# A graph layer on one core: open segments in two parts, half of the first gate moved up, six PSUM banks and the gate ahead of the numerators in the last pass

## The chip, the core and the metric

The kernel runs on one core of one Trainium2 chip. Its engines are TensorE (matrix products into PSUM, eight banks of 128 x 512 f32), VectorE, ScalarE, GpSimd and SyncE (SP), which here only issues transfers; GpSimd issues the indirect transfers and some plain ones, ScalarE some plain ones. 16 DMA engines move the data. The metric is the device time of one execution in microseconds (us). The kernel's time before is 2014.91 us, the median of three runs (2013.11 to 2015.74).

## What is computed

A graph layer over 1250 nodes of 1024 features and 20000 edges of 8 types, then a feed-forward part; all in f32.

```python
xn = _layernorm(x)
# graph part: per relation a mean over a node's edges, then a matrix
out = xn @ root + bias
for r in range(8):
    mask = (edge_type == r)
    sums = segment_sum(xn[src] * mask[:, None], dst, N)
    cnt = segment_sum(mask, dst, N)
    out = out + (sums / maximum(cnt, 1.0)[:, None]) @ weight[r]
u = out
z = concatenate([u, xn], axis=1) @ w_gate + b_gate
gnn = tanh(u) * z + xn * (1.0 - z)
# mixing part: linear attention, 8 heads of 16, features 1, q, q (x) q
normed = rms_norm(xn, gamma); q, k, v = normed @ w_q, normed @ w_kv
mix = ((phi(q) @ (phi(k).T @ v)) / maximum(phi(q) @ sum(phi(k)), 1e-5)) @ w_out
x = x + gnn + mix
# feed-forward part with FP4 quantized operands (blocks of 16)
xq = quant(_layernorm(x))
h = silu(xq @ quant(f_gate).T) * (xq @ quant(f_up).T)
x = x + quant(h) @ quant(f_down).T
```

## The kernel before

The nodes are worked in ten blocks (`NB`) of 128 rows (`BR`), the last of 98. The features are worked in two halves of 512 columns (`HD`). All of it is unrolled; each engine takes its instructions in a fixed order that a scheduler made of the program.

1. Up to about 1483 us: layer norm, sorting of the edges by node (L224 to L391), and the products of all nodes with all relation matrices, `y_d` in DRAM, then `root_d`, `gx_d` (the second half of the gate's product, with `xn`) and `qkv_d`. Beside the products run the messages.
2. A message tile (`message`, L604; `gather`, L459; `segments`, L466) is 128 sorted edges: GpSimd gathers 128 rows of `y_d` (four `msg` buffers), ScalarE and VectorE weight them and split them into two parts (`hi`, `lo`), TensorE sums equal nodes with two products (L477, L478), ScalarE copies the sum (L479) and writes it to `seg_d` (L480). There are 157 tiles (`ST`) for each half. The second half has 23 gathers left when the products end.
3. The end of the messages (the loop at L835): beside the last ones stand the sums of the mixing part (`mix_sums`, `mix_pairs`, ending in `bd`, L743), `open_rows` (which tile's last row belongs to a node that goes on in the next tile), and `open_segments` (L805), which adds these last rows to the row of the tile in which the node ends: row 127 of each tile is loaded (`last_rows`, L797; 128 rows in `s1`, 29 in `s2`), multiplied by a selection (`osel`), evacuated (`osum`) and added in DRAM by an indirect transfer (L813), in two pieces of 128 and 29 rows. For half 0 that is done among the messages, for half 1 after them (L859). `behind` (L827) is a list of loads on GpSimd's queue: `x`, `root`, `gx` of block 0, the 4 MB of `wg`, the same three of block 1; one is taken after each step from the fourth on. `FW` = 6 quantized weight tiles are loaded meanwhile, on ScalarE's queue.
4. The numerators (`mix_num`, L663): for a block, `q` transposed, four products with `bd` (L673) into four PSUM tiles, each multiplied and reduced on VectorE (L676, L678), a fifth product (L680, L681), and the division (L690); `mix_transposed` (L693) turns the result. `FIRST` = 4 of them are made before block 0, among the transposes of the weights (`ffn_weight`, L817).
5. `block(b)` (L869): the node rows `u` are gathered from both halves of `seg_d` (`nodes`, L658), `root_d` is added (L887, L896), `u` is transposed (L160, copies L90), the gate is 16 products (L893, L904), the mixing part's output two (L907); then the sum, layer norm and quantizing (`x1`, `x2`). Block 0 takes the halves apart. `hidden` (L921) and `finish` (L938) are the feed-forward part. The last pass (L950) runs, for each i, a numerator ahead, `block(i)`, `hidden(i-1)`, `finish(i-2)`.

PSUM: `sg`, two banks, for messages (`sm_tile`); `mm`, four banks (`mm_tile`) for all products; `tr`, two banks for transposes. `tc.issue_after(ins)` keeps what follows behind `ins` on its engine. `loaded[b]` has two buffers for each of `xt`, `rt`, `gx` and `u`.

Of the kernel before, what the change touches and what calls it, by code (L numbers as in the profile page):

```python
# [8 lines left out]
F32 = mybir.dt.float32  # L9
# [18 lines left out]
FIRST = 4  # L28
LAG = 2
EARLY = 140  # L30
FW = 6
SUMS = 7
# [17 lines left out]
def gps_layer(ctx: ExitStack, tc: tile.TileContext, x, src, dst, et, w_rel, w_root, bias,  # L50
# [9 lines left out]
    def psum_pools(stack, **bufs):  # L60
        for name, n in bufs.items():
            psum[name] = stack.enter_context(tc.tile_pool(name=f"ps_{name}", bufs=n, space=PSUM))
# [12 lines left out]

    def mm_tile():
        return psum["mm"].tile([128, 512], F32, name="mm")
# [388 lines left out]
    def segments(nh, t, msg):  # L466
# [13 lines left out]
        S.dma_start(seg_d[nh][t * 128:(t + 1) * 128, :], seg)  # L480
# [29 lines left out]
    psum_pools(ctx, sg=2)  # L510
# [123 lines left out]
    qn = mx.tile([BR, NB, 128], F32, name="qn")  # L634
# [64 lines left out]

    with ExitStack() as late:  # L700
        op = late.enter_context(tc.tile_pool(name="op", bufs=1))
        pb = late.enter_context(tc.tile_pool(name="pb", bufs=4))
        fw = late.enter_context(tc.tile_pool(name="fw", bufs=6))
        kv = op.tile([BR, NB, 257], F32, name="kv")
# [3 lines left out]
        for o, c0, c in ((kv, 128, 384), (qn, 0, 128)):  # L708
            nc.sync.dma_start(o[:, :NB - 1, :c - c0], qkv_d[:full, c0:c].rearrange("(b p) c -> p b c", p=BR))
            nc.sync.dma_start(o[:rest_n, NB - 1, :c - c0], qkv_d[full:, c0:c])  # L710
# [86 lines left out]
        def last_rows(nh):  # L797
            s1 = op.tile([128, HD], F32, name="s1")
            s2 = op.tile([128, HD], F32, name="s2")
            rows127 = seg_d[nh][:ZERO, :].rearrange("(t p) c -> t p c", p=128)[:, 127, :]  # L800
            G.dma_start(s1, rows127[:128])
            G.dma_start(s2[:B2], rows127[128:])
            return s1, s2

        def open_segments(nh, s1, s2):  # L805
            for i, n in enumerate((128, B2)):
                ps = mm_tile()
                T.matmul(ps[:n], osel[:, 0, i * 128:i * 128 + n], s1, start=True, stop=(i == 0))
                if i == 1:
                    T.matmul(ps[:n], osel[:B2, 1, 128:], s2[:B2], start=False, stop=True)  # L810
                osum = op.tile([128, HD], F32, name="osum", bufs=2)
                evac(osum[:n], ps[:n])
                G.indirect_dma_start(  # L813
                    out=seg_d[nh][:, :], out_offset=bass.IndirectOffsetOnAxis(ap=orow[:n, i:i + 1], axis=0),
                    in_=osum[:n, :], in_offset=None, compute_op=ALU.add)
# [16 lines left out]
        rest = [mix_sums, open_rows, lambda: open_segments(0, *last_rows(0))]  # L832
        rest += [lambda b=b: mix_pairs(b) for b in range(NB)]
        done = EARLY
        for i, p in enumerate(rest):  # L835
# [4 lines left out]
            if i >= 3:  # L840
                behind.pop(0)()
                if len(there) < FW:
                    there.append(ffn_weight(S, *weights[len(there)]))
# [9 lines left out]
        with tc.issue_after(gathered_last[0]):  # L853
            for b in range(2):
                nodes(b, 0)
            rows = last_rows(1)
        for p in steps[:SUMS]:
            p()
        open_segments(1, *rows)  # L859
# [9 lines left out]
    def block(b):  # L869
# [13 lines left out]
        if b == 0:  # L883

            for nh, cs in halves:
                with tc.issue_after(first_nums if nh else gathered_last[0]):
                    V.tensor_tensor(u[:, cs], rt[:, cs], u[:, cs], ALU.add)  # L887
                transpose_cols(uT[:, nh * 4:nh * 4 + 4, :], u[:, cs], n, D_CHUNKS[:4], 0)
                for mh, ms in halves:
                    if nh == 0:  # L890
                        gates.append(mm_tile())
                    for k in range(4 * nh, 4 * nh + 4):
                        T.matmul(gates[mh][:n], uT[:, k, :n], wg[:, k, ms], start=(k == 0), stop=(k == KC - 1))  # L893
# [97 lines left out]
```

## Time and profile before

| | |
|---|---|
| runs, median of three | 2014.91 us |
| profiled execution, whole / span | 2007.39 / 2005.6 us |
| mean granted TensorE clock | 0.968 |
| busy, share of the span | TensorE 95%, VectorE 65%, ScalarE 37%, GpSimd 30% |
| last gather of a message issued | 1561.92 us |
| last write of `seg_d` by ScalarE | 1574.13 us |
| `bd` made (L743) | 1572.16 + 0.69 us |
| block 0: last gate product ends | about 1626.2 us |
| `hidden` of block 0 / 1 / 2 / 3 begins (transposes of `x2`) | 1664.17 / 1699.06 / 1740.15 / 1781.05 us |
| span after the last gate of block 9 | 50.5 us |

A row of the timeline is start, length, engine, line, operation, tiles out and in, shapes, count; in brackets how long the engine stood idle before it and what ended that. An f32 product of 128x512 shows as two rows (x16 are eight products). A wait for several things is put down to the one that came last by the profile, which can be the wrong one where a transfer is among them. TensorE rows are modelled, so busy shares of TensorE say less than its gaps.

### The profile page before, as it was taken

What the parts mean: (1) busy time and instruction counts of PE and PEld (TensorE: products, weight loads), DVE (VectorE), ACT (ScalarE), POOL (GpSimd) and SP (SyncE); (2) the same over time, 40 slices, a digit from 0 to 9 for tenths busy, and PEclk for the clock granted to TensorE, in tenths of its full rate; (3) what the DMA queues carried; (4) which work ended last, traced back from release to release, by engine and by line L of the source; (5) the groups of instructions that cost most, each with busy time, mean ns of one, the idle gap of its engine ahead of it and who ended that gap; (6) DMA issues with size and microseconds to landing.
All of it is one profiled execution on the core that took longest, in us unless ns stands there. A gap on an engine that the chain in (4) does not pass through costs nothing. (4 is left out here: it accounts for less than half of the span.)

```text
span 2005.6 us, 24060 instructions
## 1 busy us (share of the span) xinstructions
PE 1900.6 (95%) x7828; PEld 1283.0 (64%) x7828; DVE 1310.8 (65%) x2931; ACT 751.3 (37%) x1302; POOL 611.6 (30%) x590
## 2 busy tenths in 40 slices
PE   8999999999999999999999989989988889989998
PEld 5465447787777777777777866767653334444544
DVE  8988946767646455645554675675656776676665
ACT  5111421112234545555554555555543332222311
POOL 1022588884012322332323334233344201000100
PEclk9999999999999999999999989999887879999999
DMA  6265334444346767677767677778688521211100
GB/s 215 79 160 150 77 89 125 115 117 124 120 155 212 229 220 232 215 236 226 227 212 221 222 252 254 235 235 263 227 302 305 146 80 55 76 63 61 56 21 29
DMA packets 159256, 332.76 MB, mean 166 GB/s; under 512 B 27006, under 2 KB 35876, under 8 KB 159130
## 3 DMA queue, kind: packets, MB, share of 16 engines
q0 software_dynamic: 39616, 112.32, 21.4%
q10 hardware_dynamic: 77370, 142.68, 19.2%
q1 hardware_dynamic: 42144, 76.22, 12.0%
q8 instruction: 62, 1.02, 0.2%
q14 instruction: 64, 0.52, 0.1%
HBM read 184.42 MB, written 146.53 MB: 165 GB/s over the span
## 5 line engine op out<-in xcount | busy, mean ns | idle before, releaser
L546 PE MATMUL ab<-wH,xH 128*128 128x512 f32 (+2 forms) x1440 | 568.0, 395 | 2.0 <-ACT wH L505 2.0
L547 PE MATMUL ab<-wL,xL 128*128 128x512 f32 (+2 forms) x1440 | 564.6, 393 | 0.0
L548 PE MATMUL ab<-wD,xD 128*128 128x512 f32 (+2 forms) x1440 | 561.2, 394 | 2.6 <-DVE wD L507 1.9
L461 POOL DMA_INDIRECT msg<-y_d,key x314 | 318.6, 1014 | 675.0 <-PE sm L478 337.5
L474 DVE SCALAR_TENSOR_TENSOR msg<-msg,weight,hi 128x512 fp32r<-128x512 f32 x314 | 234.4, 750 | 135.9 <-ACT hi L472 77.6
L548 PEld LDWEIGHTS ab<-wD,xD 128*128 128x128 f32 (+1 forms) x1440 | 268.2, 187 | 74.6 <-DVE wD L507 10.2
L546 PEld LDWEIGHTS ab<-wH,xH 128*128 128x128 f32 (+1 forms) x1440 | 269.5, 187 | 64.7 <-ACT wH L505 3.5
L547 PEld LDWEIGHTS ab<-wL,xL 128*128 128x128 f32 (+1 forms) x1440 | 269.3, 187 | 63.8 <-DVE wL L506 0.4
L479 ACT COPY seg<-sm 128x512 f32<-128x512 f32 x314 | 182.1, 584 | 204.3 <-PE sm L478 159.5
L472 ACT ACTIVATE hi<-msg,weight 128x512 fp32r<-128x512 f32 x314 | 222.1, 721 | 72.4 <-DMA msg<-y_d,key 30.0
L387 POOL DMA_INDIRECT sort_d<-pay,row x160 | 211.0, 1319 | 60.8 <-issue 48.4
L554 ACT ACTIVATE yt<-ab 128x512 f32<-128x512 f32 (+2 forms) x180 | 106.0, 592 | 320.9 <-PE ab L547 275.7
L555 DVE SCALAR_TENSOR_TENSOR yt<-ab,yt 128x512 f32<-128x512 f32 (+2 forms) x180 | 121.8, 681 | 155.7 <-ACT yt L554 148.2
L405 PE MATMUL mm<-wt,xnT 128*128 128x512 f32 (+1 forms) x480 | 221.3, 603 | 0.0
L478 PE MATMUL sm<-msg,sel 128*128 128x512 f32 x314 | 137.4, 438 | 24.2 <-DVE msg L474 24.0
L477 PE MATMUL sm<-hi,sel 128*128 128x512 f32 x314 | 133.2, 428 | 26.2 <-ACT hi L472 20.3
L470 DVE TENSOR_SCALAR sel<-iota_n,last_row 128x128 fp32r<-128x128 f32 x314 | 89.4, 287 | 103.8 <-PE sm L478 98.8
L405 PEld LDWEIGHTS mm<-wt,xnT 128*128 128x128 f32 (+1 forms) x480 | 85.5, 188 | 86.6 <-issue 86.3
L505 ACT CAST wH<-h 128x512 fp32r<-128x512 f32 x144 | 88.5, 621 | 123.5 <-DVE h L504 112.3
L904 PE MATMUL mm<-wg,uT 128*128 128x512 f32 (+1 forms) x288 | 131.6, 611 | 0.2 <-ACT uT L90 0.2
L506 DVE TENSOR_TENSOR wL<-raw,h 128x512 fp32r<-128x512 f32 x144 | 98.3, 683 | 27.2 <-PE mm L405 27.2
L659 POOL DMA_INDIRECT u<-seg_d,node_at x20 | 25.6, 1281 | 276.3 <-issue 244.8
(276 smaller groups left out, 2100.3 us busy)
## 6 DMA issues: line engine op xcount, KB each, us to landing
seg_d<-seg ACTq DMA_DIRECT2D x314, 256.0 KB
y_d<-yt ACTq DMA_DIRECT2D x144, 256.0 KB
raw<-in_L_gnn_weight_dram SPq DMA_DIRECT2D x104, 256.0 KB
db<-in_dst_dram POOLq DMA_DIRECT2D x32, 305.2 KB
xt<-in_x_dram SPq DMA_DIRECT2D x16, 512.0 KB
wt<-in_L_gnn_weight_dram SPq DMA_DIRECT2D x24, 256.0 KB
msg<-y_d,key POOLq DMA_INDIRECT x314
lb<-lo_d POOLq DMA_DIRECT2D x32, 156.2 KB
```

What stands on the lines that cost most here:

```text
L387: st = G.indirect_dma_start(out=sort_d[:, :], out_offset=bass.IndirectOffsetOnAxis(ap=row[:, t:t + 1], axis=0), in_=pay[:, t, :], in_offse ...
L405: T.matmul(ps[:n], xnT[:, k, block_rows(b)], held[k], start=(k == 0), stop=(k == KC - 1))
L461: gathered_last[0] = G.indirect_dma_start(out=msg[:, :], out_offset=None, in_=y_d[nh][:, :], in_offset=bass.IndirectOffsetOnAxis(ap=key[:, ...
L472: S.mul(hi, msg, weight[:, t:t + 1])
L474: V.scalar_tensor_tensor(lo, msg, weight[:, t:t + 1], hi.bitcast(F32), op0=ALU.mult, op1=ALU.subtract)
L477: T.matmul(ps, sel, hi, start=True, stop=False)
L478: T.matmul(ps, sel, lo, start=False, stop=True)
L479: S.copy(seg, ps)
L546: T.matmul(pa[:p, :n], xH[:, k, ns], Wh[:, :n], start=(k == 0), stop=False)
L547: T.matmul(pa[:p, :n], xL[:, k, ns], Wl[:, :n], start=False, stop=(k == KC - 1))
L548: T.matmul(pb[:p, :n], xD[:, k, ns], Wd[:, :n], start=(k == 0), stop=(k == KC - 1))
L904: T.matmul(gates[nh][:n], uT[:, k, :n], wg[:, k, cs], start=(k == 0), stop=(k == KC - 1))
```

## The change

- PSUM: the pool of the messages (`sg`) stands on the other side; after block 0 it is closed and its two banks become a pool `more`; from then on every third `mm_tile` comes from it.
- `qn` and `kv` become one tile `qkv`, loaded by two transfers instead of four; it stays to the end. `FW` 6 to 5, `FIRST` 4 to 3, `SUMS` 7 to 5.
- The open segments: `open_first` adds the piece of 128 rows for both halves among the messages; the adds to half 1 and the writes of tiles beyond 128 are declared independent. `open_rest` adds the piece of 29 rows (its last row is zero, 28 are loaded); for half 1 that is all that is left after the messages.
- `gate_first`: after `open_rest(1)`, the first half of block 0's `u` is added, transposed and multiplied with its half of `wg`, into the two `sg` banks; `block(0)` adds the second half.
- The loads in `behind` stay behind the message gathered last.
- Last pass: `block(i)` stands ahead of the numerator; the numerators are 3 to 9, one behind each of blocks 1 to 7.

```diff
-FIRST = 4
+FIRST = 3
-FW = 6
-SUMS = 7
+FW = 5
+SUMS = 5
...
+    banks = [0]
+
     def mm_tile():
-        return psum["mm"].tile([128, 512], F32, name="mm")
+        banks[0] += 1
+        return psum["more" if "more" in psum and banks[0] % 3 == 0 else "mm"].tile([128, 512], F32, name="mm")
...
-        S.dma_start(seg_d[nh][t * 128:(t + 1) * 128, :], seg)
+        wrote = S.dma_start(seg_d[nh][t * 128:(t + 1) * 128, :], seg)
+        if nh == 1 and t > 128:
+            tc.declare_no_dep(wrote.ins, group="open", reason="these are added to rows of tiles up to 128, and of waste")
...
-    psum_pools(ctx, sg=2)
+    sums = ctx.enter_context(ExitStack())
+    psum_pools(sums, "right", sg=2)
...
-    qn = mx.tile([BR, NB, 128], F32, name="qn")
+    qkv = mx.tile([BR, NB, 385], F32, name="qkv")
+    qn, kv = qkv[:, :, :128], qkv[:, :, 128:]
...
+    first_gates = []
+
+    def gate_half(nh, u, uT):
+
+        n, cs = BR, halves[nh][1]
+        transpose_cols(uT, u[:, cs], n, D_CHUNKS[:4], 0)
+        for ps, (_, ms) in zip(first_gates, halves):
+            for k in range(4):
+                T.matmul(ps[:n], uT[:, k, :n], wg[:, 4 * nh + k, ms], start=(nh + k == 0), stop=(nh + k == 4))
+
+    def gate_first():
+
+        first_gates.extend(sm_tile() for _ in range(2))
+        _, rt, _, u = loaded[0]
+        with tc.issue_after(gathered_last[0]):
+            V.tensor_tensor(u[:, :HD], rt[:, :HD], u[:, :HD], ALU.add)
+        gate_half(0, u, mx.tile([128, 4, BR], F32, name="uT0"))
...
-        for o, c0, c in ((kv, 128, 384), (qn, 0, 128)):
-            nc.sync.dma_start(o[:, :NB - 1, :c - c0], qkv_d[:full, c0:c].rearrange("(b p) c -> p b c", p=BR))
-            nc.sync.dma_start(o[:rest_n, NB - 1, :c - c0], qkv_d[full:, c0:c])
+        nc.sync.dma_start(qkv[:, :NB - 1, :384], qkv_d[:full, :].rearrange("(b p) c -> p b c", p=BR))
+        nc.sync.dma_start(qkv[:rest_n, NB - 1, :384], qkv_d[full:, :])
...
-        def last_rows(nh):
-            s1 = op.tile([128, HD], F32, name="s1")
-            s2 = op.tile([128, HD], F32, name="s2")
-            rows127 = seg_d[nh][:ZERO, :].rearrange("(t p) c -> t p c", p=128)[:, 127, :]
-            G.dma_start(s1, rows127[:128])
-            G.dma_start(s2[:B2], rows127[128:])
-            return s1, s2
-
-        def open_segments(nh, s1, s2):
...
+        s1, s2 = {}, [op.tile([128, HD], F32, name=f"s2{nh}") for nh in range(2)]
+        for nh in range(2):
+            V.memset(s2[nh][:B2], 0.0)
+
+        def open_add(nh, i, n, ps):
+            osum = op.tile([128, HD], F32, name="osum", bufs=2)
+            evac(osum[:n], ps[:n])
+            return G.indirect_dma_start(
+                out=seg_d[nh][:, :], out_offset=bass.IndirectOffsetOnAxis(ap=orow[:n, i:i + 1], axis=0),
+                in_=osum[:n, :], in_offset=None, compute_op=ALU.add).ins
+
+        def open_first(nh):
+            s1[nh] = op.tile([128, HD], F32, name="s1")
+            G.dma_start(s1[nh], rows127(nh)[:128])
+            ps = mm_tile()
+            T.matmul(ps, osel[:, 0, :128], s1[nh], start=True, stop=True)
+            added = open_add(nh, 0, 128, ps)
+            if nh == 1:
+                tc.add_to_no_dep_group("open", added)
+
+        def open_rest_rows(nh):
+
+            G.dma_start(s2[nh][:B2 - 1], rows127(nh)[128:ST - 1])
+
+        def open_rest(nh):
+            ps = mm_tile()
+            T.matmul(ps[:B2], osel[:, 0, 128:], s1[nh], start=True, stop=False)
+            T.matmul(ps[:B2], osel[:B2, 1, 128:], s2[nh][:B2], start=False, stop=True)
+            open_add(nh, 1, B2, ps)
...
-        rest = [mix_sums, open_rows, lambda: open_segments(0, *last_rows(0))]
+        rest = [mix_sums, open_rows, lambda: (open_first(0), open_rest_rows(0), open_rest(0), open_first(1))]
...
-                behind.pop(0)()
+                with tc.issue_after(gathered_last[0]):
+                    behind.pop(0)()
...
-            rows = last_rows(1)
+            open_rest_rows(1)
         for p in steps[:SUMS]:
             p()
-        open_segments(1, *rows)
+        open_rest(1)
+        gate_first()
...
         if b == 0:
-
-            for nh, cs in halves:
...
+            gates = first_gates
+            with tc.issue_after(first_nums):
+                V.tensor_tensor(u[:, HD:], rt[:, HD:], u[:, HD:], ALU.add)
+            gate_half(1, u, uT)
...
     for i in range(NB + 2):
-        if 0 < i and i + FIRST <= NB:
-            if i + FIRST < NB:
-                mix_num(i + FIRST)
-            mix_transposed(i + FIRST - 1)
         if i < NB:
             ahead[i] = block(i)
         if i == 0:
-            mix_num(FIRST)
-            mix_transposed(FIRST - 1)
+            sums.close()
+            psum_pools(ctx, "right", more=2)
+        if i and i + FIRST - 1 < NB:
+            mix_num(i + FIRST - 1)
+        if i and i + FIRST - 2 < NB:
+            mix_transposed(i + FIRST - 2)
```

More of the change, by code (lines that the diff above doesn't have):

```diff
@@ L58, in gps_layer, with psum_pools @@
     psum = {}
-    def psum_pools(stack, **bufs):
+    def psum_pools(stack, side="left", **bufs):
         for name, n in bufs.items():
-            psum[name] = stack.enter_context(tc.tile_pool(name=f"ps_{name}", bufs=n, space=PSUM))
+            psum[name] = stack.enter_context(tc.tile_pool(name=f"ps_{name}", bufs=n, space=PSUM, side=side))
     HD = D // 2
@@ L702, in gps_layer @@
         pb = late.enter_context(tc.tile_pool(name="pb", bufs=4))
-        fw = late.enter_context(tc.tile_pool(name="fw", bufs=6))
-        kv = op.tile([BR, NB, 257], F32, name="kv")
+        fw = late.enter_context(tc.tile_pool(name="fw", bufs=FW))
         V.memset(kv[:, :, 256:257], 1.0)
         full, rest_n = (NB - 1) * BR, N - (NB - 1) * BR
-        for o, c0, c in ((kv, 128, 384), (qn, 0, 128)):
-            nc.sync.dma_start(o[:, :NB - 1, :c - c0], qkv_d[:full, c0:c].rearrange("(b p) c -> p b c", p=BR))
-            nc.sync.dma_start(o[:rest_n, NB - 1, :c - c0], qkv_d[full:, c0:c])
+        nc.sync.dma_start(qkv[:, :NB - 1, :384], qkv_d[:full, :].rearrange("(b p) c -> p b c", p=BR))
+        nc.sync.dma_start(qkv[:rest_n, NB - 1, :384], qkv_d[full:, :])
         def mix_sums():
@@ L795, in open_rows, with rows127 @@
             V.tensor_copy(orow, row_f[:, 3])
-        def last_rows(nh):
-            s1 = op.tile([128, HD], F32, name="s1")
-            s2 = op.tile([128, HD], F32, name="s2")
-            rows127 = seg_d[nh][:ZERO, :].rearrange("(t p) c -> t p c", p=128)[:, 127, :]
-            G.dma_start(s1, rows127[:128])
-            G.dma_start(s2[:B2], rows127[128:])
-            return s1, s2
-        def open_segments(nh, s1, s2):
[L806 to L815, printed above, removed]
+        def rows127(nh):
+            return seg_d[nh][:ZERO, :].rearrange("(t p) c -> t p c", p=128)[:, 127, :]
@@ L883, in block @@
         if b == 0:
-            for nh, cs in halves:
[L886 to L893, printed above, removed]
+            gates = first_gates
+            with tc.issue_after(first_nums):
+                V.tensor_tensor(u[:, HD:], rt[:, HD:], u[:, HD:], ALU.add)
+            gate_half(1, u, uT)
         else:
```

## The prediction

> **What bounds the kernel now.** I read the busy table in stretches first. Its columns: stretch, its length, busy time (and instruction count) of TensorE, weight loads, VectorE, ScalarE and GpSimd, then granted TensorE clock, DMA share and GB/s.
>
> ```profile
> 1482.80:1525.50 42.70, 30.99 (x88) 16.11 (x88) 22.29 (x72) 15.96 (x27) 16.14 (x20) 0.66 0.98 368
> 1525.50:1572.90 47.40, 42.64 (x125) 11.82 (x124) 35.36 (x65) 18.78 (x32) 23.56 (x21) 0.91 0.81 251
> 1572.90:1626.20 53.30, 46.21 (x160) 20.56 (x160) 30.77 (x66) 17.26 (x40) 6.44 (x5) 0.87 0.33 94
> 1626.20:1955.10 328.90, 308.88 (x911) 158.13 (x910) 229.75 (x400) 84.21 (x122) 21.27 (x16) 0.95 0.17 56
> 1955.10:2005.60 50.50, 41.52 (x125) 21.61 (x123) 25.83 (x46) 8.48 (x16) 0.00 (x0) 0.93 0.08 29
> ```
>
> Up to about 1482.8 us the compiled order of the two kernels is the same on every engine, so only these 523 us can move. They are: the last 23 messages, first with the transfers full (0.98), then less full (0.81); the passage from messages to nodes, 1572.9 (`bd` is made) to 1626.2 (block 0's gate is summed); the pass over blocks; the tail of 50.5 us. TensorE is busy 94% of the pass at clock 0.95, so some 6% of that and the slow clock are to be had there.
>
> Second, TensorE's timeline where a numerator (`mix_num`) stands in the pass:
>
> ```profile
> 1675.13 0.27 PE L697 MATMUL tr<-ident,num 128*128 128x128 f32 x1
> 1675.70 1.13 PE L673 MATMUL mm<-bd,qT 32*128 32x512 f32 x6 [0.30 <-ACT qT L668]
> 1677.89 1.12 PE L673 MATMUL mm<-bd,qT 32*128 32x512 f32 x2 [1.05 <-DVE hs L933]
> 1679.85 0.71 PE L680 MATMUL mm<-rl,qT 128*128 128x264 f32 x2 [0.84 <-DVE prod L676]
> 1680.49 0.49 PE L681 MATMUL mm<-crow,ones 1*128 1x136 f32 x2
> ```
>
> The fourth L673 waits until VectorE has read an `mm` bank (L933), L680 for the next (L676): four banks for five outputs. Third, the chain of waits at blocks without a numerator:
>
> ```profile
> 1856.16 0.45 PE tr L160 x4
> ...
> 1889.17 0.45 PE tr L160 x4
> ...
> 1922.18 0.45 PE tr L160 x4
> ...
> 1955.08 0.45 PE tr L160 x4
> ```
>
> Such a block costs 33.0 us, nearly all TensorE. Blocks 2, 3 and 4, with a numerator, took 41.3, 40.8 and 41.3 (their `u` transposes start at 1680.92, 1722.19, 1763.03 and 1804.29).
>
> Fourth, GpSimd and VectorE in the passage:
>
> ```profile
> 1577.91 0.58 POOL L802 DMA_DIRECT2D s<-seg_d  x1 [11.43 <-DMA seg_d<-seg]
> 1587.32 1.69 POOL L813 DMA_INDIRECT seg_d<-osum,orow  x1 [8.84 <-ACT osum L90]
> 1593.17 2.15 POOL L813 DMA_INDIRECT seg_d<-osum,orow  x1 [4.17 <-ACT wguT L90]
> 1602.70 1.04 POOL L659 DMA_INDIRECT u<-seg_d,node_at  x1 [7.38 <-DVE prod L676]
> ```
> ```profile
> 1594.90 0.69 DVE L676 TENSOR_TENSOR prod<-mm,qn 128x512 f32<-128x512 f32 x1 [7.25 <-PE mm L673]
> ...
> 1601.59 0.29 DVE L690 TENSOR_TENSOR num<-num,den 128x128 f32<-128x128 f32 x1
> 1608.70 0.68 DVE L887 TENSOR_TENSOR u<-rt,u 128x512 f32<-128x512 f32 x1
> ```
>
> The two adds to `seg_d` go one after the other: 5.9 us from the first's issue to the second's, 9.5 from there to the node gather. The releasers named there, a weight copy and a product, have nothing to do with `seg_d` in the code; what fits is the landing of the add before. `u` is added at 1608.7, after the fourth numerator, though TensorE held VectorE up for 7.25 us in between.
>
> **The change part by part.**
>
> *The pass, six banks and gate first.* TensorE's work for one numerator, from its rows at 1627.08 without a bank wait: two transposes and the `qT` copy 0.7, four L673 1.14, L680 and L681 1.1, together 2.95 us. A block's transposes and gates are 16.0, `hidden` 11.1 (transposes and copy 1.4, L929 9.73), `finish` 5.9 (L945 5.42): 33.0. From block 0's gate to `hidden` of block 8 the changed order has nine blocks' gates, eight `hidden`, seven `finish` and seven numerators (FIRST 3 moves one in): 144 + 88.8 + 41.3 + 20.7 = 294.8. Each output now reuses the bank of six outputs before. Counted from the last gate matmul of a block: the fourth L673's bank was read long ago, L680's is read by L905 at 0.9 while L680 comes at about 3, and `hidden`'s first needs L908 (2.9) and comes at 5.2. So the bank waits go to zero. VectorE has 28 us of work (27.9 and 28.2 busy in blocks 3 and 4) in a block of 36.
>
> What is late next is the first block. Its `x2` needs, after the gate: L905 twice and L909, 2.9; then in VectorE's compiled order block 2's `u` add, for which the gather needs 7.1 from the end of L909 (1665.5 to 1672.6 before), 10.0; that add and block 1's first L905 and L908, 12.8; root, reciprocal and ScalarE's L917, 15.1; quantizing 8.4 with three operations of block 1 (2.7) between, 26.2. TensorE fills 18.9 of it (block 1's transposes and gates 16, numerator 2.95). A hole of 7.5 remains, and a hole leaves a slow clock: after the idle stretch before 1645 the gate of block 1 took 8.68 for x16 instead of 7.03, its transposes 1.91 instead of 1.04; 2.5 in all. Sum 294.8 + 10 = 305 against 328.9: **-24** (bounds -28, no hole, and -5, the banks still bind).
>
> *The passage.* From `bd` the numerators set the pace: VectorE needs 7.0 us for each (1594.90 to 1601.88), first product 1.8 after `bd`. Numerator 0 with the half `u` add ends at +9.5. TensorE meanwhile has numerator 0 (to +3.7), the two `osel` matmuls (a bank by +4.6; 0.86 each at full clock, from L904's x16 in 7 us; 1.7 to 3.4 at half), transposes and copy 1.1, half a gate 6.9: +14.6 to +18. Numerator 1's first product +16.3 to +19.5, its end +23.5 to +26.5; 27 transposes limited by ScalarE's copies 4.4 (x8 take 1.33), numerator 2 from about +25.8 to +35.8; the `u` add, transposes, copy 1.8; second half gate 6.9: gate summed at +41.4 to +44.5. I take 43 against 53.4 now: **-10** (-12 to -9). The adds hide behind this: the rest rows' matmuls by +8, copy 0.6, one add instead of two 5.9 to 9.5, gather 6: `u` lands by +17 to +25, and is wanted at +33. If that cover were gone, each us past +33 is one us. The first add, its 128-row matmul and evacuation run among the messages, where TensorE and VectorE have gaps (30.99 busy of 42.7).
>
> *The messages.* `wg` (4 x 1 MB) and the six `x`, `root`, `gx` loads (3 MB) leave the full stretch and come among or behind the last eight gathers. The two stretches move 15.7 and 11.9 MB now (GB/s by length); some 5.5 MB change over, so the second gets 17.4 MB, 44 us at the 395 GB/s seen from 1495 to 1520: it fits into its 47.4, and the first gets slack. GpSimd also takes three adds and two row loads in line there; `s1` has one buffer, so its second load waits for the first's matmuls, with gathers queued behind it. Early gain and late loss: **0** (-8 to +8: eight gathers at 3.6 instead of 2.7 us is +7, the first stretch at its later pace -8).
>
> *At nothing:* one `qkv` load for two (VectorE waits 5.05 us for `kv` now; 0.6 MB more is +1.5 us, 1.5 MB of other loads gone is -4; inside the bound above); two memsets of 29 rows, in VectorE's idle stretches before `kv` lands; SUMS 5, which only keeps the second part of the open sums behind numerator 0; FW 5 (a load more on SP, ready before its transposes, which come behind numerator 1; if it is late, its landing, some 2 us, is lost once).
>
> Sum 0 - 10 - 24 = -34. The profiled execution (span 2005.6, whole 2007.4) would come to a span of 1971.6; the runs' median is 2014.9, 7.5 over that execution, so I predict 2014.9 - 34 = 1981.
>
> **The rivals.**
> *A, banks still bind* (the change does not do what it says: six in name, but two of them wait for the first gates' readers and for slots). For: the waits on L933 and L676 above. Against: the `sm` banks are read once, early. Ring of four in the new order: L673 0.9, L680 0.6, `hidden` 1.3 late, 2.7 x 7 = 19: 2000.
> *B, the loads hold up the last messages.* Eight gathers +7, three adds in line +4, no early gain: +11, 1992. For: at DMA share 0.98 gathers came 3.6 us apart. Against: 17.4 MB fit. The Trainium skill, "DMA: Bandwidth & Descriptors", section "SWDGE vs HWDGE vs iDMA", speaks for B: GpSimd's transfers have one queue, which takes turns with the hardware queues inside each DMA engine. By it every late gather stands behind the `wg` load before it; at half of 395 GB/s 4.2 MB and eight gathers would take 31 us instead of 21.5, nearly B's price. No run here shows it yet.
> *A and B together:* -34 + 30, 2011.
> *C, slower: the gather ahead of the quantizing.* In the new order VectorE meets the next block's `u` add before it quantizes the present one. The gather lands 6.3 us after issue now, and VectorE gets there 8 after; it has 6 to 8 us of slack a block. Past 14 us after issue each us is lost in eight blocks; from 18.3 the gain is gone. At 20: +48 - 34, 2029. For: VectorE waits 3.6 us for this gather today, and each block has 1.5 MB of loads beside it. Against: DMA share 0.18 there.
>
> **How the numbers follow.** Forecast 0.62, A 0.13, B 0.14, both 0.04, C 0.07. The forecast's own range is -50 (all good ends) to -20. Below 1965 I leave 0.05, above 2002 some 0.11 (C and both): 1965 to 2002. 0.2% is 4 us, what a measurement tells from none: forecast, A and B are faster, 0.89; both is the same, 0.04; C slower, 0.07.
>
> **What would show it.** Right: gather and second `u` add waiting no longer for the adds, TensorE without bank waits at L673 and L680, 36 us a block with a numerator, one hole before `hidden` of block 0 with half clock after. Wrong: last message later than 1572 us, 38 us or more a block, or VectorE idle before L896 in every block.

## The result, and the profile after

The changed kernel takes 1985.57 us, the median of four runs (1983.85 to 1989.09), against 2014.01 us for the kernel before on the same chip (four runs, 2012.92 to 2015.74). The ratio is 0.9855, with an interval from 0.983 to 0.9879: 28 us, some 1.4%, are gained. The prediction was 1981 us. The profiled execution is the run of 1983.85 us, span 1982.1.

First the busy table in stretches of the changed kernel, to set beside the one in the prediction. Its columns are again stretch, length, busy time (and count) of TensorE, weight loads, VectorE, ScalarE and GpSimd, granted TensorE clock, DMA share and GB/s. The five stretches end at the same events as before (the first add to `seg_d`, `bd`, block 0's gate, the last block's gate, the end), but for the third: the prediction's table ends it at the gate's last product on TensorE (1626.2), this one at the gate's sum on VectorE, which came 0.9 us after that product in the kernel before.

```profile
1485.80:1523.00 37.20, 25.41 (x83) 14.39 (x83) 21.90 (x73) 14.78 (x25) 13.93 (x13) 0.68 0.76 259
1523.00:1577.97 54.97, 43.94 (x131) 12.87 (x130) 36.79 (x67) 20.73 (x37) 30.13 (x29) 0.84 0.97 333
1577.97:1622.20 44.23, 36.61 (x154) 18.72 (x155) 26.04 (x54) 16.60 (x38) 4.69 (x4) 0.96 0.35 106
1622.20:1934.20 312.00, 293.42 (x913) 150.99 (x912) 231.54 (x413) 80.60 (x121) 18.43 (x16) 0.98 0.18 59
1934.20:1982.10 47.90, 38.49 (x126) 20.08 (x124) 25.94 (x47) 8.39 (x16) 0.00 (x0) 0.98 0.08 31
```

The full DMA (0.98) has moved from the first stretch to the second (0.97), as the loads did, and the second has become longer (47.4 to 55.0). By the same end the passage is 10 us shorter (the lengths show 9); the pass is 17 us shorter. Second, a numerator in the pass, on TensorE:

```profile
1787.17 1.02 PE L940 MATMUL mm<-wo,mixT 128*128 128x512 f32 x2
1788.03 0.27 PE L673 MATMUL tr<-ident,qkv 128*128 128x128 f32 x1
...
1788.66 1.14 PE L680 MATMUL mm<-bd,qT 32*128 32x512 f32 x8 [0.25 <-ACT qT L675]
1789.73 0.71 PE L687 MATMUL mm<-rl,qT 128*128 128x264 f32 x2
1790.37 0.49 PE L688 MATMUL mm<-crow,ones 1*128 1x136 f32 x2
1790.80 1.09 PE L163 MATMUL tr<-ident,x 128*128 128x128 f32 x8
1793.51 0.86 PE L962 MATMUL mm<-wguT,xqT 128*128 128x352 f32 x2 [1.62 <-ACT xqT L93]
```

L680 and L687 (L673 and L680 before) wait for no bank any more: the numerator takes 2.8 us (1788.03 to 1790.80), close to the 2.95 of the prediction's sum. But the last line shows a wait that the prediction doesn't have: 1.62 us for ScalarE's copies of `xqT`, ahead of `hidden`. Third, ScalarE at that place, with one VectorE line that it names:

```profile
1791.75 1.24 ACT L919 ACTIVATE sx<-xt,xf 128x1024 f32<-128x1024 f32 x1 [2.98 <-DVE x L944]
1792.90 1.05 ACT L93 COPY xqT<-tr 128x512 f32<-128x512 f32 x2
```
```profile
1790.50 1.21 DVE L944 TENSOR_TENSOR x<-sx,gx 128x1024 f32<-128x1024 f32 x1
```

ScalarE stands 2.98 us at the `sx` activation of a later block until VectorE's L944 has read the old `sx` (there are two buffers), then takes 1.24 for it, and only then copies `xqT`, whose transposes ended 1 us earlier. Fourth, the passage: GpSimd, then VectorE and TensorE.

```profile
1581.23 0.56 POOL L846 DMA_DIRECT2D s<-seg_d  x1 [10.77 <-issue]
1585.42 2.17 POOL L831 DMA_INDIRECT seg_d<-osum,orow  x1 [3.63 <-ACT osum L93]
1594.71 1.00 POOL L666 DMA_INDIRECT u<-seg_d,node_at  x1 [7.12 <-DMA seg_d<-osum,orow]
```
```profile
1596.48 0.69 DVE L683 TENSOR_TENSOR prod<-mm,qkv 128x512 f32<-128x512 f32 x1 [9.83 <-PE mm L680]
```
```profile
1586.12 8.03 PE L715 MATMUL sm<-wg,uT 128*128 128x512 f32 x16
```

One add instead of two, 9.3 us ahead of the gather; VectorE idle 9.83 us ahead of numerator 1 because TensorE has the half gate (8.03 us) in front of it. VectorE adds `root` to the second half of `u` at 1611.91, at once after the last numerator (1611.70), with no wait.

In what follows four stages are read from one profiled execution of each kernel: from the issue of the `qkv` load on SP to the end of `bd` (messages); to the end of the second gate sum of block 0 (passage); to the first product of `hidden` of block 8 (pass); to the end (tail). "Period" is the time from one `hidden` to the next in a block with a numerator; the clock is the mean granted TensorE clock over the passage.

| kernel | load issued at | messages | passage | its clock | pass | tail | period |
|---|---|---|---|---|---|---|---|
| before | 1482.9 | 90.0 | 54.3 | 0.87 | 329.1 | 49.4 | 40.9 to 41.1 |
| before_sx3 | 1487.5 | 89.6 | 59.2 | 0.71 | 331.8 | 49.3 | 41.1 to 42.2 |
| changed | 1485.8 | 92.2 | 44.2 | 0.96 | 313.3 | 46.6 | 37.16 |
| after_again | 1494.4 | 94.6 | 46.6 | 0.89 | 314.2 | 49.5 | 37.16 |
| sx3 | 1492.1 | 94.9 | 46.9 | 0.89 | 302.6 | 48.6 | 35.83 |
| sx3_again | 1488.9 | 90.3 | 45.2 | 0.92 | 303.5 | 47.0 | 35.83 |
| banks4 | 1488.2 | 92.9 | 46.2 | 0.93 | 316.1 | 48.3 | 37.68 |
| sx3_banks4 | 1487.3 | 93.5 | 46.0 | 0.93 | 315.7 | 48.4 | 37.68 |
| oldorder | 1490.7 | 93.0 | 44.3 | 0.96 | 311.6 | 48.1 | 36.7 to 37.5 |
| nogate | 1489.5 | 93.6 | 51.5 | 0.77 | 311.6 | 46.9 | 37.16 |
| sx3_early | 1496.0 | 94.7 | 44.5 | 0.96 | 301.8 | 48.2 | 35.83 |
| sx3_split | 1489.7 | 96.6 | 46.3 | 0.93 | 302.5 | 48.1 | 35.83 |
| sx3_whole | 1488.6 | 95.1 | 47.4 | 0.89 | 302.3 | 48.3 | 35.83 |
| sx3_w5 | 1491.8 | 91.8 | 56.4 | 0.79 | 302.2 | 48.3 | 35.82 |

The second column is read first: up to the load the kernels do the same work, and yet it is issued anywhere from 1482.9 to 1496.0. Single totals differ by as much for no reason of the change, while the periods of one kernel agree to some 0.1 us, but for `oldorder` and for single blocks at a lower clock. So a step is judged by its stage; the medians, whose intervals are some 5 us either way, check it. The passage needs its clock beside it: where its program is the same, it takes 44.2 to 44.5 us at a granted clock of 0.96, 45.2 to 46.3 at 0.92 and 0.93, 46.6 and 46.9 at 0.89; and the kernel before, with the same passage in both executions, takes 54.3 at 0.87 and 59.2 at 0.71.

### The profile page after: what moved, and what is told of

Same layout as the page of the kernel before. It is cut to its first block, busy times and chain, and to the rows that moved or that the text cites. A ratio compares the mean times of both kernels' runs of the same rounds, so it can differ in the third digit from the quotient of the medians.

```text
span 1982.1 us, 24076 instructions
## 1 busy us (share of the span) xinstructions
PE 1869.1 (94%) x7828; PEld 1272.4 (64%) x7828; DVE 1308.5 (66%) x2934; ACT 747.7 (38%) x1299; POOL 617.0 (31%) x590
## 3 DMA queue, kind: packets, MB, share of 16 engines
q1 hardware_dynamic: 40976, 76.42, 12.4%
## 5 line engine op out<-in xcount | busy, mean ns | idle before, releaser
L464 POOL DMA_INDIRECT msg<-y_d,key x314 | 329.5, 1049 | 662.6 <-PE sm L481 333.6
L481 PE MATMUL sm<-msg,sel 128*128 128x512 f32 x314 | 137.0, 436 | 24.4 <-DVE msg L477 24.4
L473 DVE TENSOR_SCALAR sel<-iota_n,last_row 128x128 fp32r<-128x128 f32 x314 | 89.6, 287 | 99.0 <-PE sm L481 94.7
L937 PE MATMUL mm<-wg,uT 128*128 128x512 f32 (+1 forms) x288 | 126.4, 592 | 0.0
L962 PE MATMUL mm<-wguT,xqT 128*128 128x352 f32 (+1 forms) x320 | 101.2, 476 | 10.7 <-ACT xqT L93 10.7
```

What stands on the lines that cost most here:

```text
L464: gathered_last[0] = G.indirect_dma_start(out=msg[:, :], out_offset=None, in_=y_d[nh][:, :], in_offset=bass.IndirectOffsetOnAxis(ap=key[:, ...
L481: T.matmul(ps, sel, lo, start=False, stop=True)
L937: T.matmul(gates[nh][:n], uT[:, k, :n], wg[:, k, cs], start=(k == 0), stop=(k == KC - 1))
L962: T.matmul(ps[:n, :I], xqT[:, k, :n], wguT[:, k, i * I:(i + 1) * I], start=(k == 0), stop=(k == KC - 1))
```

## The experiments

**The missing 11 us of the pass: a third buffer for `sx`.** In the changed kernel:

```diff
-        sx = wk.tile([BR, D], F32, name="sx", bufs=2)[:n]
+        sx = wk.tile([BR, D], F32, name="sx", bufs=3)[:n]
```

> The changed kernel with three buffers for sx instead of two. Theory S: in each block with a numerator, ScalarE's next sx activation (L919) waits some 3 us for VectorE's x sum (L944) to free its buffer, and the xqT copies queued behind it hold TensorE 1.62 us ahead of hidden (L962). With a third buffer the activation runs long before, the wait ahead of L962 falls to about 0.3 us, the period of a block with a numerator falls from 37.16 to some 35.8, and seven of them give -9: 1976 against 1985.6. Rival 1: the xqT copies are late for another reason, or VectorE (its x sum and norm) becomes the next bound: period stays at 37, 1985. Rival 2: sx now stands ahead of the qT copy and waits there for its own load of xt: numerators start late, 1990 or more.

Measured: 1982.67 us (five runs), ratio 0.9818 (0.9793 to 0.9843); period 35.83, pass 302.6. TensorE and ScalarE at the same place:

```profile
1797.59 1.09 PE L163 MATMUL tr<-ident,x 128*128 128x128 f32 x8
1798.97 1.45 PE L962 MATMUL mm<-wguT,xqT 128*128 128x352 f32 x4 [0.29 <-ACT xqT L93]
```
```profile
1788.97 1.24 ACT L919 ACTIVATE sx<-xt,xf 128x1024 f32<-128x1024 f32 x1 [6.42 <-DMA xt<-in_x_dram]
1795.13 0.27 ACT L675 COPY qT<-tr 128x128 f32<-128x128 f32 x1 [4.92 <-PE tr L673]
1798.34 1.07 ACT L93 COPY xqT<-tr 128x512 f32<-128x512 f32 x2 [2.77 <-PE tr L163]
```

The activation now waits for nothing but its own load, is done 4.9 us before ScalarE is wanted for `qT`, and the copy follows the transposes. The wait falls from 1.62 to 0.29 and the period by 1.33, as expected: theory S holds, and both rivals fall (for rival 2 that load would have to land 5 us later still). The median is 7 us above the 1976 that was expected; by the ratio it is 7 us below the changed kernel. To set the two beside each other on one chip they were run once more, together:

> The changed kernel as it is, once more, on the chip of this call, to stand beside the third sx buffer. Theory: periods of 37.16 in blocks with a numerator again, a stage from the qkv load's issue to bd of 92 to 95, ratio to before 0.983 to 0.988. If the stage or the periods differ from the first execution's, the readings made from that one do not hold.

> The changed kernel with three sx buffers, once more, beside the changed kernel itself. Theory S: 9 to 11 us less than it (seven stalls of 1.35, and a shorter first period), ratio to before 0.979 to 0.982. Rival: what the pass gains is lost again in other stages, difference under 3 us.

Measured: 1990.37 us (1984.68 to 2001.06) and 1979.97 us (1976.74 to 1985.47), ratios 0.9864 (0.9831 to 0.9897) and 0.9833 (0.9799 to 0.9867). The intervals overlap; the difference of the medians is 10.4 us, that of the pass 10.7 in both pairs of executions. By its pass, the kernel with the third buffer is the fastest of these.

**Does the kernel before have the same stall?** The same edit in the kernel before.

> The kernel before the change with three sx buffers. Theory: in its pass the sx activation stands behind the xqT copies where there is a numerator, so that the third buffer finds no stall to remove: 41.0 us a block as before, ratio 0.998 to 1.002. Rival: the buffer helps there too, 1.35 us in each block, ratio 0.994 to 0.995. Its messages are those of the kernel before, so it is also a second execution of them: from the load's issue to bd 90.0 again if the changed messages really cost 2 to 5 us, 92 to 95 if the first execution of before was only a lucky one.

Measured: 2015.9 us against 2014.75, ratio 1.0002 (0.9982 to 1.0022), period 41.1 but for the first (42.2). The buffer is worth nothing there: the stall came with the change, since with the gate first the next `sx` stands ahead of the copies of `xqT` on ScalarE. In the kernel before it stands behind them:

```profile
1740.84 1.07 ACT L90 COPY xqT<-tr 128x512 f32<-128x512 f32 x2 [15.16 <-PE tr L160]
1743.39 1.24 ACT L880 ACTIVATE sx<-xt,xf 128x1024 f32<-128x1024 f32 x1 [1.48 <-DVE x L911]
```

Its messages take 89.6 us, so the 90.0 of before repeats.

**Banks and order, each alone.** Four banks with the new order, and six with the old one:

```diff
-        return psum["more" if "more" in psum and banks[0] % 3 == 0 else "mm"].tile(...)
+        return psum["mm"].tile(...)
```

> The changed kernel with the new order of the pass, but all outputs in the four mm banks (the two of more are never used). Theory (prediction's rival A priced alone): bank waits of some 2.7 us come back in each of seven blocks with a numerator, +19: 2005. Since ScalarE's late xqT copy already costs 1.35 us of those, which a bank wait at the same place would cover, the sum may be 7 x 1.35 = 9 less: 1995. Rival: the order alone brought the gain and the banks nothing: 1986.

```diff
+        if i > 1 and i + FIRST - 1 < NB:
+            mix_num(i + FIRST - 1)
+        if i > 1 and i + FIRST - 2 < NB:
+            mix_transposed(i + FIRST - 2)
         if i < NB:
             ahead[i] = block(i)
...
-        if i and i + FIRST - 1 < NB:
+        if i == 1 and i + FIRST - 1 < NB:
...
-        if i and i + FIRST - 2 < NB:
+        if i == 1 and i + FIRST - 2 < NB:
```

> The changed kernel with six banks, but from the second block on the numerators stand ahead of the block's gate, as before the change. Theory: the banks did it, the order is worth little: bank waits stay away at L680 and L687, and the pass is within 4 us of the changed kernel's: 1982 to 1990. Rival: the order is needed, since the numerator's VectorE work then stands ahead of the gate's sums, and x2 of the block before comes late for hidden: 2 to 3 us in each of seven blocks, 2000 to 2006.

Measured: 1994.52 us, ratio 0.9891 (0.9866 to 0.9915), pass 316.1; and 1991.81 us, ratio 0.9882 (0.986 to 0.9904), pass 311.6. From 329.1 before, the order alone saves 13.0, the banks alone 17.5, and both together 15.8 (each with one numerator more in the pass than before): with two `sx` buffers the new order brings nothing beside the six banks. `oldorder` is as its theory has it, without bank waits at L680 and L687 and with a pass within 4 us, though its median is 2 us over the range expected; `banks4` comes to the lower of the two figures expected, 1995. What hides behind that is in the rows. Four banks, new order:

```profile
1796.58 1.13 PE L680 MATMUL mm<-bd,qT 32*128 32x512 f32 x6 [0.25 <-ACT qT L675]
1797.96 1.12 PE L680 MATMUL mm<-bd,qT 32*128 32x512 f32 x2 [0.25 <-DVE sx L941]
...
1800.08 1.09 PE L163 MATMUL tr<-ident,x 128*128 128x128 f32 x8
1801.47 0.55 PE L163 MATMUL tr<-ident,hq 128*128 128x128 f32 x3 [0.29 <-ACT xqT L93]
```

The bank wait is 0.25, not 1.05 as before the change: with the gate first, the bank was read earlier. But it parts the fourth product from the other three. With six banks the four take 1.14 together; here three take 1.13 and the fourth 1.12 by itself, so that L687 begins 2.43 us after the first L680, and not 1.07 as above. These 1.36 us hide the late copy. ScalarE's rows are those of the changed kernel:

```profile
1799.67 1.24 ACT L919 ACTIVATE sx<-xt,xf 128x1024 f32<-128x1024 f32 x1 [2.98 <-DVE x L944]
1800.83 1.08 ACT L93 COPY xqT<-tr 128x512 f32<-128x512 f32 x2
```

In both kernels the copy begins 5.73 us after the last L940; the transposes that it copies begin 4.98 us after it here, 3.63 there. Six banks, old order:

```profile
1815.23 1.14 PE L680 MATMUL mm<-bd,qT 32*128 32x512 f32 x8
1816.30 0.71 PE L687 MATMUL mm<-rl,qT 128*128 128x264 f32 x2
...
1818.61 0.66 PE L163 MATMUL tr<-ident,u 128*128 128x128 f32 x4 [0.48 <-ACT mixT L705]
1819.67 1.13 PE L940 MATMUL mm<-wo,mixT 128*128 128x512 f32 x2 [0.40 <-DVE prod L683]
```

Its bank waits are gone at L680 and L687 too (0.40 is left at L940). So each edit removes most of the old waits, and each is still 1 to 2 us a block above the 35.83 of the third buffer. Whether the banks are worth anything beside the third buffer was asked with both edits in one kernel:

> The changed kernel with three sx buffers and all outputs in the four mm banks. Theory: with four banks the compiled order puts other transposes between x's transposes and hidden, which covered the late copy already; the third buffer then brings nothing more and the period stays at 37.7, so that the two extra banks are worth 1.8 us a block beside the third buffer, against 0.5 without it: 9 to 13 us over sx3_again in all. Rival: the period falls to 36 or less and the extra banks are worth nothing.

Measured: 1995.2 us, ratio 0.9908 (0.9874 to 0.9941), pass 315.7, period 37.68 to the hundredth as without the buffer. So in the new order, with four banks the buffer saves nothing (316.1 to 315.7), and with two buffers the two banks save 2 to 3 us (316.1 to 313.3 and 314.2); both together save 12.6 to 13.5. Banks and buffer pay only as a pair. The theory's figure is right; its cause, other transposes ahead of `hidden`, is the smaller part (the three of `hq` take 0.3 us more there), and the parted product the larger (1.36 of the 1.85 a block). The old order with the third buffer wasn't tried.

**The half gate.** The first half of block 0's gate back in block 0:

```diff
-        gate_first()
         for p in steps[SUMS:]:
...
+            first_gates.extend(sm_tile() for _ in range(2))
             gates = first_gates
-            with tc.issue_after(first_nums):
-                V.tensor_tensor(u[:, HD:], rt[:, HD:], u[:, HD:], ALU.add)
-            gate_half(1, u, uT)
+            for nh, cs in halves:
+                with tc.issue_after(first_nums if nh else gathered_last[0]):
+                    V.tensor_tensor(u[:, cs], rt[:, cs], u[:, cs], ALU.add)
+                gate_half(nh, u, uT if nh else wk.tile([128, 4, BR], F32, name="uT0"))
```

> The changed kernel with the first half of block 0's gate back in block 0, behind all numerators in the program. Theory G (the prediction's way of counting): half a gate with its transposes and copy, some 8 us of TensorE, is no longer hidden behind the numerators and comes on the path: passage 43 becomes 49 to 51, 1992 to 1994. Rival: in the changed kernel VectorE stands idle 9.8 us ahead of numerator 1 because TensorE is at the half gate, so that the half gate is on the path anyway; undone, the numerators end about 9 us earlier and the half gate costs its 7 to 8 behind them: no difference, 1984 to 1987.

Measured: 1990.43 us, ratio 0.9866 (0.9842 to 0.9891), passage 51.5. Both halves now stand behind the last numerator:

```profile
1605.53 2.09 PE L680 MATMUL mm<-bd,qT 32*128 32x512 f32 x8
...
1619.87 14.00 PE L715 MATMUL sm<-wg,uT 128*128 128x512 f32 x32 [1.00 <-ACT uT L93]
```

The last numerator's products begin 22.5 us after `bd` (1583.05), against 25.9 (1603.84 less 1577.97) with the half gate in front of them: 3.4 us earlier, not the 9 of the rival. From there to the gate it takes 14.3 us (1605.53 to 1619.87) against 10.6 (1603.84 to 1614.44), at a granted clock of 0.65 against 1.00, and the gate of 14.0 instead of 7.03 costs 7 more: 7.3 in all. So in this execution the passage is as theory G has it (51.5 against 44.2 to 46.9, 5 to 7 us), but half of the 7.3 lies in a stretch at a slower clock. Whether the slower clock belongs to the edit isn't shown: the passage has 0.77 here, 0.89 to 0.96 with the half gate up, and the kernel before had 0.87 and 0.71 in two executions. The medians show less, a ratio of 0.9866 against 0.9855 and 0.9864 of the changed kernel, 2 us at most. What moving the half gate up is worth stays open between 0 and 7 us.

**The open segments.** Both pieces of half 1 behind the messages again (with three `sx` buffers, as in the next three):

```diff
-        if nh == 1 and t > 128:
-            tc.declare_no_dep(wrote.ins, group="open", ...)
...
-lambda: (open_first(0), open_rest_rows(0), open_rest(0), open_first(1))]
+lambda: (open_first(0), open_rest_rows(0), open_rest(0))]
...
+            s1[1] = op.tile([128, HD], F32, name="s1")
+            G.dma_start(s1[1], rows127(1)[:128])
             open_rest_rows(1)
...
+        ps = mm_tile()
+        T.matmul(ps, osel[:, 0, :128], s1[1], start=True, stop=True)
+        open_add(1, 0, 128, ps)
         open_rest(1)
```

> The changed kernel with three sx buffers, and the open segments of the second half added whole behind the messages again: both loads of last rows, both matmuls and both adds come behind the last message. Theory (the prediction's cover): u is wanted when the last numerator ends, 34 us after bd; with two adds in a row (5.9 us from the first issue to the second, 9.3 from there to the gather, 6 for the gather) it lands 1 to 4 us after that, so the passage of 44 to 47 grows by 1 to 4, and the messages gain 0 to 2 for one add less in GpSimd's queue: ratio within 0.002 of the other kernels of this call with the same pass, 0.981 to 0.984. Rival: the adds stand in the path as before the change, passage +10, 53 to 56: ratio 0.986 to 0.988.

Measured: 1983.45 us, ratio 0.983 (0.9807 to 0.9853), passage 47.4. GpSimd, and VectorE's add:

```profile
1589.98 1.70 POOL L829 DMA_INDIRECT seg_d<-osum,orow  x1 [2.37 <-DMA s<-seg_d]
1596.94 2.13 POOL L829 DMA_INDIRECT seg_d<-osum,orow  x1 [5.26 <-issue]
1606.80 1.03 POOL L664 DMA_INDIRECT u<-seg_d,node_at  x1 [7.73 <-DVE kq L689]
```
```profile
1618.15 0.69 DVE L928 TENSOR_TENSOR u<-rt,u 128x512 f32<-128x512 f32 x1
```

The gather goes out 23.1 us after `bd` (1583.68) instead of 16.7, and still VectorE doesn't wait for it at +34.5. The adds never come back into the path; the passage of 47.4 stands beside 44.2 to 46.9 in the kernels that split the adds. Splitting the open segments is worth 0 to 3 us in this kernel, no more than executions of one program differ by (at the same clock, 0.89, two of them took 46.6 and 46.9).

**The messages.** The loads early again, and the `k` and `v` columns by a load of their own:

```diff
-                with tc.issue_after(gathered_last[0]):
-                    behind.pop(0)()
+                behind.pop(0)()
```

> The changed kernel with three sx buffers, and the loads of wg, x, root and gx may again be issued among the last gathers as early as their place in the program gives (no ordering behind the last gathered message). Stage to read: from the issue of the qkv load to bd, 90.0 before the change, 92.1 to 94.9 (mean 93.3) in five executions of the changed messages. Theory L (prediction's rival B: the loads hold up the last messages): the stage comes back by 3 to 5 us, to 88 to 91, and the time falls by as much, ratio to before 0.979 to 0.981. Rival Q: the merged qkv load costs it (first product 13.0 to 13.7 us after the load's issue, 10.0 before the change), so the stage stays at 92 to 95. Rival N: loads early slow the gathers while the transfers are full, stage 95 or more.

```diff
-        nc.sync.dma_start(qkv[:, :NB - 1, :384], qkv_d[:full, :]...)
-        nc.sync.dma_start(qkv[:rest_n, NB - 1, :384], qkv_d[full:, :])
+        for o, c0, c in ((kv, 128, 384), (qn, 0, 128)):
+            nc.sync.dma_start(o[:, :NB - 1, :c - c0], qkv_d[:full, c0:c]...)
+            nc.sync.dma_start(o[:rest_n, NB - 1, :c - c0], qkv_d[full:, c0:c])
```

> The changed kernel with three sx buffers, and the k and v columns loaded first and the q columns by a load of their own, as before the change. Theory Q: the first product comes about 10 us after the load's issue instead of 13, and, since the pair products run through to bd, the stage from the load to bd falls by 3 us to 89 to 92. Rival L: the first product comes earlier, but bd waits for the last messages, and these for the loads: the first product earlier by 3, the stage unchanged at 92 to 95, time unchanged within 2 us.

Measured: 1980.93 us, ratio 0.9818 (0.9796 to 0.9841), messages 94.7; and 1987.16 us, ratio 0.9861 (0.9841 to 0.9881), messages 96.6. Neither brings the stage back. Theory L fails. Q gets no support, but the split is no clean test of it: VectorE's first product of `k` and `v` came 15.8 us after the first load's issue, later than with one load (13.7 in the changed kernel). It still waited for a landing in `qkv`, probably because both loads fill one tile. What the early loads do is read off the last gather of a message on GpSimd:

| kernel | load issued to last gather | last gather to `bd` |
|---|---|---|
| before, before_sx3 | 79.0, 78.5 | 10.9, 11.1 |
| nine with the changed messages, mean (range) | 79.8 (77.4 to 81.3) | 13.2 (12.4 to 14.8) |
| sx3_early | 86.3 | 8.4 |
| sx3_split, sx3_whole | 84.7, 79.8 | 11.9, 15.3 |

With the loads behind, the last gather goes out within 1 us of its time before, on the mean, and what follows it is 2.2 us longer; with the loads in front it goes out 7 us later, and 2.6 of these come back behind it. That is rival N in kind, though its stage of 95 or more was just missed. How the late loads cost time shows where ScalarE stands idle until a gather lands, here for the last gather but two, before and in the changed kernel:

```profile
1556.93 1.79 POOL L461 DMA_INDIRECT msg<-y_d,key  x1 [1.34 <-PE sm L477]
1562.31 0.72 ACT L472 ACTIVATE hi<-msg,weight 128x512 fp32r<-128x512 f32 x1 [2.16 <-DMA msg<-y_d,key]
```
```profile
1558.80 1.27 POOL L464 DMA_INDIRECT msg<-y_d,key  x1 [2.25 <-PE sm L481]
1568.10 0.72 ACT L475 ACTIVATE hi<-msg,weight 128x512 fp32r<-128x512 f32 x1 [2.09 <-DMA msg<-y_d,key]
```

From issue to use this gather takes 5.4 us before and 9.3 with the loads of `wg` among the gathers. `sx3` and `sx3_early` differ in nothing but the place of the loads, and show 8.6 and 5.8. So the late loads do hold up the gathers that follow them, by some 3 us. The changed kernel pays at the one end what the early loads pay at the other.

**Numerator 1 ahead of the half gate.** An attempt at the 9.83 us of VectorE's idle time: numerators 0 and 1, then the half gate, then numerator 2, with 15 of the 20 weights' transposes behind that.

```diff
-SUMS = 5
+SUMS = 6
+GATE = 8
+W_AT = (0, 5, 5, 20)
...
-            for w in range(len(weights) * b // FIRST, len(weights) * (b + 1) // FIRST):
+            for w in range(W_AT[b], W_AT[b + 1]):
...
+        for p in steps[SUMS:GATE]:
+            p()
         gate_first()
-        for p in steps[SUMS:]:
+        for p in steps[GATE:]:
             p()
```

> The changed kernel with three sx buffers, and another order of the passage: numerators 0 and 1, then the first half gate, then numerator 2, and 15 of the 20 weights' transposes behind that. Theory: in the changed kernel VectorE stands idle 9.8 us ahead of numerator 1 because TensorE is at the half gate; with numerator 1 ahead of it VectorE has work meanwhile, the three numerators end 8 us earlier, and the passage, then bounded by TensorE's own work of some 39 us, falls from 44 to 47 to 38 to 41: ratio 0.978 to 0.979. Rival: the weights' transposes, now all together ahead of the second half gate, wait for their loads (5 slots) or for ScalarE's copies, and the passage stays at 44 to 47.

Measured: 1991.37 us, ratio 0.9862 (0.9838 to 0.9885), passage 56.4, longer by 10. TensorE:

```profile
1591.21 1.90 PE L853 MATMUL mm<-s,osel 29*29 29x512 f32 x2 [0.77 <-DMA s<-seg_d]
1593.04 4.92 PE L682 MATMUL mm<-bd,qT 32*128 32x512 f32 x8
...
1601.83 9.49 PE L717 MATMUL sm<-wg,uT 128*128 128x512 f32 x16 [0.46 <-ACT uT L95]
...
1627.32 0.88 PE L165 MATMUL tr<-ident,fw 128*128 128x128 f32 x3 [2.64 <-DMA fw<-fdn_d]
```
```profile
1612.40 0.69 DVE L685 TENSOR_TENSOR prod<-mm,qkv 128x512 f32<-128x512 f32 x1 [9.78 <-PE mm L682]
```

VectorE's idle time wasn't removed, only moved, from ahead of numerator 1 to ahead of numerator 2 (9.78), because the half gate is in front of that one now. Numerator 1's products also began only at 1593.04, behind the rest rows' matmuls that wait for banks and a load, and took 4.92 instead of 1.14, at a granted clock of 0.50 from 1593.04 to 1601.83; and the transposes, gathered at the end, wait for their loads (2.64 for the last), the wait that the rival names. But the rival's figure, 44 to 47, is missed as well. The edit moves the gate and the transposes at once, so what each of them costs isn't shown.

## Why the prediction was right, point by point

The forecast was -34 against a span of 2005.6; the profiled spans differ by 23.5 (messages and what lies ahead of them +5.1, passage -10.0, pass -15.8, tail -2.8), the medians by 28.4. The time lies inside the range and nearer to the forecast than to any rival; the second set of the same kernel (1990.37) lies nearer to B's 1992. The tail was not forecast, and `after_again` (49.5) doesn't repeat its gain.

- *Pass, predicted -24, measured -15.8.* The mechanism was right: bank waits gone, one hole before `hidden` of block 0. The step that failed is "`hidden` 11.1 (transposes and copy 1.4, L929 9.73)" as part of the 36 us period: the transposes and copy took 2.71 (1790.80 to 1793.51), since ScalarE's queue held the next `sx` in front of the copy and that waited for VectorE. In the kernel before, that copy came with nothing in front of it (1740.84, shown above), and the prediction carried its 1.4 over into an order in which a different instruction stands before it. With the third buffer it is 1.38 (1797.59 to 1798.97), and the pass is 302.6 to 303.5, where the prediction has 305. The 10.7 us come from 1.33 in each of five whole periods, 1.6 to 2.6 in the first (33.61 against 31.01 and 31.98), and one `hidden` at a lower clock (below).
- *The first block's hole.* Predicted: `x2` quantized 26.2 after the gate, 2.5 more for a slow clock. Measured: its transposes begin at 1646.59, 24.4 after the gate's sum, and the rows around the hole are

```profile
1641.39 0.71 PE L687 MATMUL mm<-rl,qT 128*128 128x264 f32 x2 [2.42 <-DVE gx L938]
...
1646.59 1.97 PE L163 MATMUL tr<-ident,x 128*128 128x128 f32 x8 [4.06 <-DVE x L155]
```

  The hole has two parts, 2.42 and 4.06, where the prediction has 7.5 in one. The transposes and `hidden` took 1.97 and 11.92 instead of 1.09 and 9.73, 3.1 more: right within a microsecond.
- *Passage, predicted -10 (43 us), measured -10.0 (44.2).* Numerator 1's first product came 18.5 after `bd` (predicted 16.3 to 19.5), the second `u` add 33.9 after (33). The cover that the prediction names, numerators over the adds, is real: it holds even with both adds behind the messages (sx3_whole). That the number fits to the tenth is luck: the clock of the passage was 0.96 against 0.87 before, and at 0.89 (after_again, sx3) the gain is 7 to 8 us; in this stage the prediction reckons with half clock for the two `osel` matmuls alone. The half gate's part lies between 0 and 7 us (nogate); what one numerator fewer (`FIRST` 3) is worth was not tried alone.
- *Messages, predicted 0 (-8 to +8), measured +2.2 in the stage* (+5.1 with the 2.9 us by which the load came later, where both kernels do the same work). Over nine executions of the changed messages, those of the runs that leave them as they are, the stage is 90.3 to 94.9, mean 93.0, against 90.0 and 89.6: some 3 us lost. The size was inside the bounds. The table of the last gather puts it behind the last gathers, and the pair `sx3` and `sx3_early` shows that the loads make these land later. That all of the 3 us come from there is argued; putting the loads back early moved the cost and didn't remove it. The prediction's sign of being wrong, a last message later than 1572 us, can't be read in absolute time: the last gather was issued at 1565.17 here and at 1574.19 in `after_again`, whose load came 8.5 us later as well.
- *Rival A, banks still bind:* false as put, no wait at L680 or L687 in the pass but in the first block, where L687 waits 2.42 for a bank that VectorE's L938 reads late (shown above). Priced at 2.7 us a block, four banks in fact cost 0.5 beside two `sx` buffers and 1.85 beside three.
- *Rival B, loads hold up the last messages:* in kind, for 3 us and not 11. The last eight gathers took 22.1 us from the first's issue to the last's (1543.04 to 1565.17), 23.0 before (1538.95 to 1561.92), with all four loads of `wg` among them. The Trainium skill, "DMA: Bandwidth & Descriptors", "SWDGE vs HWDGE vs iDMA", would by the prediction's estimate from its rule have made that 31 us; the trace doesn't agree at that pace of issue. It agrees in kind with the landing, 3 to 4 us later for a gather behind such a load (9.3 against 5.4).
- *Rival C, the gather ahead of quantizing:* in the first block, where VectorE waits 4.43 us before L929 (its row names no releaser); in the later ones it waits 1.43 at most, 0.27 in the block shown above, against 3.4 to 3.8 in seven blocks before the change.

## What to carry to other kernels

When an edit changes the order of a pass, read the order of every engine that feeds the bottleneck anew, the copying one included: a duration taken from the old order (here 1.4 us for transposes and copy) holds only as long as the same instruction stands in front of it. Two limits at one place hide each other: a product parted from its fellows by 0.25 us of waiting made TensorE 1.36 us late, and so a copy that was 1.33 us late cost nothing; two banks were worth 2 to 3 us with two `sx` buffers and 12 to 13 with three. So an edit that "brings little" is to be tried again once the next wait behind it is gone. Where the part ahead of a change varies by more than the change is worth, compare stages and periods, not totals, and set the granted clock beside each stage: the same passage differed by 4.9 us with it in two executions of the kernel before.

## What was not expected of the hardware

The wait of 1.62 to 1.75 us for the copies ahead of `hidden` seems to have cost more than itself at times. In four of the 18 stalled blocks of three executions (changed, after_again, nogate) the 32 products right behind the wait ran slower, like this one:

```profile
1867.83 11.42 PE L962 MATMUL mm<-wguT,xqT 128*128 128x352 f32 x32 [1.74 <-ACT xqT L93]
```

The granted clock from 1867.83 to 1879.30 is 0.85, against 1.00 in the block before it (9.73 us). In the 36 blocks at the same place of the six executions with three buffers and six banks none was slower than 9.74. The kernel before shows it more plainly: from 1675.02 to 1680.92 TensorE stood idle 2.2 us around a numerator, in waits of 1.05 us at most, and from there to 1690.48 its clock was 0.82; at the next three numerators of its pass the clock behind them was 0.83 or 0.84 over some 9.4 us. So a part of what the bank waits cost before the change was the clock behind them. That the waits caused it is argued from these counts, not shown by an edit. "TensorE: Matmul & The Clock Gate" of the Trainium skill, Part 1, gives an idle window of some 3.4 us as what takes the clock down, and speaks of frequent shorter idle times without a figure; here half of 3.4 us went before a lower clock, though not in most blocks of the changed kernel.
